# The causal mask as GpSimd selections instead of TensorE products, two score tiles moved forward, and scatters one at a time

## The chip, the cores and the metric

One core of a Trainium2 chip runs the whole kernel in one launch. The metric is the device time of one execution in microseconds; lower is better. The core's engines are named as in the profile: PE (TensorE, matrix products, with PEld for its weight loads), DVE (VectorE), ACT (ScalarE), POOL (GpSimd) and SP, which here issues transfers.

## The reference

It is one layer of attention and one of experts, each behind a layer norm and added to its input, for 8 batches of 1024 tokens of 512 features, in float32.

```python
x = x + attention(layernorm(x))
x = x + experts(layernorm(x))

# attention, 16 heads of 32 features; t is the token's place
theta_q = x_head / (1 + |w_q|) + b_q + t * phi_q      # k alike; v without t
Q = concat(cos theta_q, sin theta_q)                   # K alike; 64 wide
V = cos theta_v + sin theta_v                          # 32 wide
scores = Q K^T / sqrt(64);  scores[key after query] = -inf
out = softmax(scores) V;  result = cos theta_out + sin theta_out

# experts: softmax router over 8, the best 2 of each token, capacity 160 per
# expert and batch (later ones are dropped)
y = relu(rows W1[e] + b1[e]) W2[e] + b2[e]             # 512 -> 2048 -> 512
result[token] = sum over its 2 experts of p * y
```

## The kernel before

**Chunks.** Attention goes through 32 chunks, `n` from 0 to 31. Batch `b` is `n // 4`, head group `c` is `n % 4`; a chunk is four heads of one batch, held as two *pairs* of two heads (the two heads of a pair lie on partitions 0 to 63 and 64 to 127). The features of chunk `n + 1` are computed by DVE and ACT while PE works on chunk `n`.

**Scores.** For a pair, the 1024 queries are cut into two halves `h` of 512. `scores(pair, h, es)` yields one score tile at a time: keys along partitions, queries along the free axis, both heads in one PSUM tile of two banks (`two_banks()`, tiles `ps_s`, of which there are three). Half 0 has three tiles: its first key block with 512 queries; a double tile, in which the key blocks with 384 and with 128 remaining queries share the 512 columns; and one of 256. Half 1 has four full tiles of 512 without a diagonal, and then the same three. Only those last three of each half (`own_keys`) contain a diagonal, and their blocks begin with it. PE makes the scores at L685. The mask is added to them by PE too: at L699 four small bfloat16 products for each such tile add a large negative number where the key lies after the query; the operands `later_b` and `keys_b` are prepared once at the start by GpSimd (L291 to L298). ACT then takes the exponential (L705) and writes the tile `e` to SBUF. The exponentials need no maximum to be subtracted.

**Products.** `attend(n, pr, h, es, halves)` multiplies the tiles `e` of one half by V (L719), tile by tile, into the PSUM tile `av`; V carries a column that gives the sum of the exponentials. After the last tile of a half DVE scales `av` into `av_sb` (L727). `turn(pr, halves, pos)` transposes the two `av_sb` of a pair on PE into a score bank (L215), and DVE divides by the sums (L754, L756) and so fills the chunk's `o_p`.

**The next chunk's features.** `qk_pre` makes the angles of queries and keys (DVE, L526, from a PSUM tile that PE transposed), `angle` wraps them (DVE, L440), ACT squares and takes sines (L444, L447, L586, L595), `times` multiplies them (DVE, L450), and transfers on SP put them into the operand `qk`. The values `v` pass L627, L632, L440 and L450. A chunk's output passes L648, L440, L450 and L659 (its addition to `x_mid`).

**Order.** The program is written in the order in which PE, ACT, DVE and SP are to run it: the helper `some(count, *gens)` takes that many steps from generators of scores (`ahead`) and products (`products`), in their turn. In the middle of a chunk come the last products of pair 0, the router's step, two score tiles of pair 1, and `turn(0, ...)`:

```python
some(NTT, *products)                        # the rest of pair 0
...
route_on(1); route_on(2)                    # the router, in head groups 1 and 2
some(2, *ahead)                             # pair 1: its first two score tiles
turn(0, halves[0], pos_n)
```

GpSimd's instructions are put in order by a scheduler, unless one is pinned with `keep_in_program_order`.

**Router and scatters.** Layer norm and router of batch `b - 1` run in pieces beside batch `b`'s chunks. They end in 16 indirect transfers, which write each token's number to its expert slot in the DRAM table `slot_d` (`scatter`, L770, issued by GpSimd). They are collected in the list `scatters`. For batches 0 to 5 all 16 are issued at one place in head group 3 of the batch that follows, each after the landing of the one before (they write the same table). `fetch_slots` (L1005) reads a finished table back.

**The seam.** After the last chunk come `experts` with the generator `ending()` as an aside: it finishes the last chunk's output, and runs the router of batch 7 while the first experts are computed. The experts' first weights W1 come in quarters; `mix_w1(i, q)` makes four differences of weight blocks (L1173), on GpSimd for the first expert's quarters 0 to 5, then `layer1` uses them in seven products (L1189) per quarter, with DVE combining the results (L1207 to L1222). The scatters of batch 6 (8 + 8) and of batch 7 (16) are issued there, with `together=True`, that is without waiting for one another, each behind the last `mix_w1` written so far.

Of the kernel before, what the change touches and what calls it, by code (L numbers as in the profile page):

```python
# [21 lines left out]
P = 128  # L22
# [43 lines left out]
REACH = [(0, -(-FIRST // CAP)), (FIRST // CAP, B)]  # L66

FAR = 1000.0 * math.sqrt(2 * DH) / (UNIT * UNIT)

# [4 lines left out]
def preln_attn_moe_kernel(  # L74
# [186 lines left out]
    before = own.tile([P, P], F32, name="before")  # L261


    keys_b = own.tile([P, 2, P], BF16, name="keys_b")
    nc.gpsimd.memset(keys_b, 0.0)
    later_b = own.tile([P, 2, P], BF16, name="later_b")
    e_row = own.tile([P, E], F32, name="e_row")
# [16 lines left out]

    later = row2.tile([P, NCH, 2 * P], F32, name="xT", bufs=1)[:, :3, :P]

    def mask():
        for part in range(2):
            for a in range(2):
                r = slice(a * 64, (a + 1) * 64)  # L290
                nc.gpsimd.tensor_copy(later_b[r, part, :], later[r, 1 + part - a, :])  # L291
                nc.gpsimd.tensor_copy(keys_b[r, part, part * 64 : part * 64 + 64], ident[r, r])

    def rest_of_loads():

        nc.gpsimd.memset(later, 0.0)
        for i in range(3):
            nc.gpsimd.affine_select(  # L298
                out=later[:, i, :], in_=later[:, i, :], compare_op=ALU.is_ge, fill=-FAR,
                base=64 * (1 - i), pattern=[[1, P]], channel_multiplier=-1,  # L300
            )
        nc.gpsimd.affine_select(
# [152 lines left out]
    def make_base(c):  # L455
# [4 lines left out]
        )  # L460
        r = room[1]
        if c > 1:
# [47 lines left out]
    def qk_pre(n):  # L510
# [3 lines left out]
        p = qkt.tile([P, 2, S], I32, name="qk_f")  # L514
        r = qkt.tile([P, 2, S], I32, name="qk_r")
        ps = two_banks()
# [159 lines left out]
    def scores(pair, h, es):  # L676

        for parts in tiles_of(h):
            n = sum(w for _, _, w, _ in parts)
            ps = two_banks()  # L680
            own_keys = parts[0][0] >= 4 * h
            for kb, q0, w, at in parts:
                for a in range(2):
                    r = slice(a * 64, (a + 1) * 64)
                    nc.tensor.matmul(  # L685
                        ps[:, a, at : at + w], lhsT=pair[r, 1, kb * P : (kb + 1) * P],
                        rhs=pair[r, 0, q0 : q0 + w], start=at == 0, stop=not own_keys,
                        skip_group_check=True,
                    )
            if own_keys:  # L690

                for part, w in ((0, 64), (1, P)):
                    for a in range(2):
                        r = slice(a * 64, (a + 1) * 64)
                        out_, late = ps[:, a, :w], later_b[r, part, :w]
                        if len(parts) == 2:
                            out_ = ps[:, a, :].rearrange("p (k q) -> p k q", q=P)[:, ::3, :w]
                            late = late.unsqueeze(1).to_broadcast([64, 2, w])
                        nc.tensor.matmul(  # L699
                            out_, lhsT=keys_b[r, part, :], rhs=late,  # L700
                            start=False, stop=part == 1, skip_group_check=True,
                        )

            e = ep.tile([P, 2, n], F32, name=f"e_{n}", bufs=8 if n == 512 else 2)
            nc.scalar.activation(  # L705
                e, ps[:, :, :n], AF.Exp, scale=UNIT * UNIT / math.sqrt(2 * DH)
            )
            es.append(e)
            yield
# [51 lines left out]

    scatters = []
    scattered = {b: [] for b in range(B)}
    mixed = []

    def scatter(count=2 * NTT * TOPK, together=False):

        for _ in range(min(count, len(scatters))):
# [5 lines left out]
            ins = queued.ins  # L774
            if together:
                tc.add_manual_dep(
# [4 lines left out]
                    reason="behind the mixture",  # L781
                )
                for other in scattered[b]:
                    tc.declare_no_dep(ins, other, reason="rows of their own")
            scattered[b].append(ins)

# [567 lines left out]
    rest_of_loads()  # L1354
    mask()
    first_stats(2, NTT)
# [14 lines left out]
    for n in range(NCK):  # L1371
# [220 lines left out]
```

## Time and profile before

| what | value |
|---|---|
| median of 4 runs | 3275.96 us (3274.84 to 3276.7) |
| profiled execution | 3271.5 us |
| its span in the profile | 3269.7 us, granted PE clock 0.997 |
| PE busy | 3190.0 us, 98% |
| DVE busy | 2254.3 us, 69% |
| ACT busy | 1323.1 us, 40% |
| POOL busy | 422.6 us, 13% |
| attention | from 0 to about 1273 us; the experts' first product starts at 1273.24 |
| L685, scores | 3072 products, 601.1 us busy |
| L719, products with V | 3072 products, 524.0 us busy |
| L699, the mask | 1536 products |
| L705, exponentials | 640, 569.6 us busy |
| L770, scatters | 128, mean 1242 ns of one |

Busy time counts overlapping matmuls once. The share of an engine is an average over attention and experts; in attention alone DVE and ACT are busier than in the whole, since the experts leave ACT nearly idle. The four chunks of a batch differ: the head group decides which layer norm and router pieces run beside it.

### The profile page before, as it was taken

How to read it: one execution, taken by the hardware profiler on the slowest of the kernel's cores; microseconds unless marked ns; L12 is line 12 of the kernel's file. 1: busy time of each engine (PE TensorE's matmuls, PEld its weight loads, DVE VectorE, ACT ScalarE, POOL GpSimd, SP SyncE). 2: the span in 40 equal slices, each digit the busy share in tenths (PEclk: the TensorE clock that was granted, in tenths of full speed). 3: DMA queues.
4: the chain of work that ended last, by engine and by line, in shares of the span. 5: the costliest groups of instructions: out<-in, count | busy, mean ns of one | idle time of the engine just before them, and what ended most of it. 6: DMA issues, size and time to landing. Idle time of an engine off the chain costs nothing.

```text
span 3269.7 us, 48752 instructions
## 1 busy us (share of the span) xinstructions
PE 3190.0 (98%) x18942; PEld 2165.8 (66%) x18942; DVE 2254.3 (69%) x4961; ACT 1323.1 (40%) x1617; POOL 422.6 (13%) x387
## 2 busy tenths in 40 slices
PE   5999999999999998999999999999999999999998
PEld 2444444444444444688688688688688688688687
DVE  8887888888788675755755755755755755855854
ACT  7888887888887873211111111211201201201201
POOL 2000202111120212311011011011011011011010
PEclk9999999999999999999999999999999999999999
DMA  5435455453545362323223222322322322322321
GB/s 163 143 98 167 135 146 147 125 156 104 181 123 160 87 175 53 116 55 83 90 50 79 93 52 76 95 52 71 101 49 71 103 47 72 104 47 70 105 42 26
DMA packets 235254, 319.74 MB, mean 98 GB/s; under 512 B 22456, under 2 KB 155280, under 8 KB 222992
## 3 DMA queue, kind: packets, MB, share of 16 engines
q1 hardware_dynamic: 211664, 273.38, 28.5%
q0 software_dynamic: 22912, 43.22, 7.1%
q8 instruction: 150, 2.46, 0.3%
q14 instruction: 80, 0.66, 0.1%
q10 hardware_dynamic: 448, 0.02, 0.0%
HBM read 187.62 MB, written 61.82 MB: 76 GB/s over the span
## 4 chain that ended last, share of the span: by engine, by line
PE 57%; DVE 0%; DMA 0%; issue 0%; POOLq 0%; POOL 0%; DVEq 0%
PE ps_p L1234 29%; PE ps_p L1189 27%; PE ps_t L1135 1%; DMA slots<-slot_d 0%; DMA out_dram<-y,slots 0%; DVE w_t L1068 0%; DVE w L1067 0%; DVE w_t L1066 0%; DVE w_t L1069 0%; POOLq L1588 0%; POOL slot_d L770 0%; POOL slots L1005 0%; DVE y L1250 0%; DVE p L1271 0%; DVE p L1272 0%
## 5 line engine op out<-in xcount | busy, mean ns | idle before, releaser
L705 ACT ACTIVATE e<-ps_s 128x1024 f32<-128x1024 f32 (+1 forms) x640 | 569.6, 938 | 195.3 <-PE ps_s L685 110.8
L685 PE MATMUL ps_s<-qk 64*128 64x512 f32 (+3 forms) x3072 | 601.1, 507 | 37.4 <-DMA qk<-qk_r 12.4
L1234 PE MATMUL ps_p<-w,hid 128*128 128x256 f32 x2560 | 568.7, 380 | 0.0
L1234 PEld LDWEIGHTS ps_p<-w,hid 128*128 128x128 f32 x2560 | 485.2, 191 | 67.0 <-DVE hid L1207 0.5
L719 PE MATMUL av<-e,v 128*64 128x512 f32 (+3 forms) x3072 | 524.0, 490 | 0.0
L1234 PE MATMUL ps_p<-w_t,hid 128*128 128x256 f32 x1920 | 430.3, 379 | 0.9 <-DVE w_t L1068 0.9
L685 PEld LDWEIGHTS ps_s<-qk 64*128 64x128 f32 x3072 | 262.5, 188 | 227.3 <-issue 110.8
L1234 PEld LDWEIGHTS ps_p<-w_t,hid 128*128 128x128 f32 x1920 | 361.3, 190 | 48.5 <-DVE w_t L1068 1.3
L719 PEld LDWEIGHTS av<-e,v 128*64 128x64 f32 x3072 | 200.6, 137 | 284.2 <-issue 268.2
L1189 PE MATMUL ps_p<-xe,w 128*128 128x256 f32 (+1 forms) x1024 | 297.8, 434 | 1.1 <-issue 1.1
L1189 PE MATMUL ps_p<-xe,t 128*128 128x256 f32 (+1 forms) x1024 | 297.1, 433 | 0.9 <-issue 0.9
L1189 PE MATMUL ps_p<-xe_s,t 128*128 128x256 f32 (+1 forms) x1024 | 296.9, 433 | 0.0
L770 POOL DMA_INDIRECT slot_d<-token,slot x128 | 159.0, 1242 | 975.5 <-issue 626.3
L1265 ACT COPY p<-ps_p 128x256 f32<-128x256 f32 x40 | 14.8, 369 | 604.8 <-PE ps_p L1234 604.7
L1189 PEld LDWEIGHTS ps_p<-xe,t 128*128 128x128 f32 x1024 | 194.3, 190 | 82.2 <-issue 1.9
L1189 PEld LDWEIGHTS ps_p<-xe,w 128*128 128x128 f32 x1024 | 193.4, 190 | 82.1 <-DVE hid L1207 3.7
L1189 PEld LDWEIGHTS ps_p<-xe_s,t 128*128 128x128 f32 x1024 | 194.3, 190 | 80.7 <-issue 0.4
L1094 POOL DMA_INDIRECT xg<-xn_d,source x76 | 74.6, 982 | 1074.4 <-PE ps_t L1135 1059.1
L1256 POOL DMA_INDIRECT out_dram<-y,slots x80 | 126.5, 1582 | 624.1 <-DVE y L1251 624.1
L1204 ACT ACTIVATE p<-ps_p,b_t 128x256 f32<-128x256 f32 (+1 forms) x128 | 65.5, 512 | 335.0 <-PE ps_p L1189 180.8
L1221 ACT ACTIVATE hid<-hid,b_more 128x256 f32<-128x256 f32 (+1 forms) x128 | 71.9, 562 | 278.7 <-DVE hid L1220 270.4
L1208 ACT ACTIVATE hid<-hid 128x256 f32<-128x256 f32 (+1 forms) x128 | 60.1, 470 | 299.3 <-DVE hid L1207 291.2
(224 smaller groups left out, 3818.5 us busy)
## 6 DMA issues: line engine op xcount, KB each, us to landing
w<-in_L_ffn_W_dram SPq DMA_DIRECT2D x256, 256.0 KB
w<-in_L_ffn_W_dram SPq DMA_DIRECT2D x64, 512.0 KB
qk<-qk_c SPq DMA_DIRECT2D x124, 256.0 KB
qk<-qk_r SPq DMA_DIRECT2D x124, 256.0 KB
qk_base<-base_d SPq DMA_DIRECT2D x28, 1024.0 KB
xn_d<-xn SPq DMA_DIRECT2D x72, 256.0 KB
x_mid<-in_L_attn_x_dram SPq DMA_DIRECT2D x16, 1024.0 KB
out_dram<-x_mid SPq DMA_DIRECT2D x8, 2048.0 KB
```

Source lines behind the costliest of these rows:

```text
L685: nc.tensor.matmul(ps[:, a, at : at + w], lhsT=pair[r, 1, kb * P : (kb + 1) * P], rhs=pair[r, 0, q0 : q0 + w], start=at == 0, stop=not own ...
L705: nc.scalar.activation(e, ps[:, :, :n], AF.Exp, scale=UNIT * UNIT / math.sqrt(2 * DH))
L719: nc.tensor.matmul(av[a * 64 : (a + 1) * 64, q0 - 512 * h :], lhsT=vt[:, kb, 2 * pr + a, :], rhs=es[i][:, a, at : at + w], start=kb == 0, ...
L770: queued = nc.gpsimd.indirect_dma_start(out=slot_d[b], out_offset=bass.IndirectOffsetOnAxis(ap=idx, axis=0), in_=src, in_offset=None,)
L1094: ins = nc.gpsimd.indirect_dma_start(out=xg, out_offset=None, in_=xn2_d[i % 2], in_offset=bass.IndirectOffsetOnAxis(ap=source[:, e, j0 + j ...
L1135: nc.tensor.transpose(ps[:, c, :], xg[:, c * P : (c + 1) * P], ident)
L1189: nc.tensor.matmul(ps, lhsT=weights[:, k, :], rhs=rows[:, k, :], start=k == 0, stop=k == 1)
L1204: nc.scalar.activation(p1, product(b11, a11), AF.Identity, bias=b1_t[:, e * NHC + q : e * NHC + q + 1])
L1208: nc.scalar.activation(h11, h11, AF.Relu)
L1221: nc.scalar.activation(h12, h12, AF.Relu, bias=more)
L1234: nc.tensor.matmul(ps, lhsT=hs[k][:, part, cols], rhs=ws[k][weight], start=k == 0, stop=k == NHQ - 1,)
L1256: ins = nc.gpsimd.indirect_dma_start(out=out, out_offset=bass.IndirectOffsetOnAxis(ap=meta[:, e, jj[r], 0:1], axis=0), in_=ys[r], in_offse ...
```

## The change

The mask leaves PE. The four products of each own tile go, with their operands and the constants made for them. After the exponential, GpSimd sets e to zero where the key lies after the query, by `affine_select` on the first 128 queries of each block, both heads at once: one selection for a plain tile, two for a double one, 4 per half, 16 per chunk, 512 in all. They are pinned in program order.

The first two score tiles of pair 1 move in front of the last three tiles of products of pair 0: `some(4, *products)`, two tiles of scores, the rest of the products. The router's steps of head groups 1 and 2 now stand directly in front of `turn(0)`.

The scatters of batches 0 to 5 are no longer issued at one place: after the last selection of each half, two of them go (if any are collected), pinned in program order. They are held back during batch 7. In the ending, batch 6's sixteen are issued as 8, 4 and 4, no longer `together`: each waits for the landing of the one before. Batch 7's sixteen stay together. Two tiles of the first chunks' features change their buffers.

```diff
-    keys_b = own.tile([P, 2, P], BF16, name="keys_b")
-    nc.gpsimd.memset(keys_b, 0.0)
-    later_b = own.tile([P, 2, P], BF16, name="later_b")
...
-    def mask():
...
-        nc.gpsimd.memset(later, 0.0)
-        for i in range(3):
-            nc.gpsimd.affine_select(
...
-        r = room[1]
+        r = qkt.tile([P, 2, S], I32, name="qk_r").bitcast(F32) if c == 2 else room[1]
...
-        r = qkt.tile([P, 2, S], I32, name="qk_r")
+        r = room[1].bitcast(I32) if n == 1 else qkt.tile([P, 2, S], I32, name="qk_r")
...
     def scores(pair, h, es):
-        for parts in tiles_of(h):
+        tiles = tiles_of(h)
+        for parts in tiles:
...
-                        rhs=pair[r, 0, q0 : q0 + w], start=at == 0, stop=not own_keys,
+                        rhs=pair[r, 0, q0 : q0 + w], start=at == 0, stop=True,
                         skip_group_check=True,
                     )
-            if own_keys:
-                for part, w in ((0, 64), (1, P)):
-                    for a in range(2):
...
-                        nc.tensor.matmul(
-                            out_, lhsT=keys_b[r, part, :], rhs=late,
-                            start=False, stop=part == 1, skip_group_check=True,
-                        )
             e = ep.tile([P, 2, n], F32, name=f"e_{n}", bufs=8 if n == 512 else 2)
             nc.scalar.activation(
                 e, ps[:, :, :n], AF.Exp, scale=UNIT * UNIT / math.sqrt(2 * DH)
             )
+            if own_keys:
+                for _, _, _, at in parts:
+                    own_ = e[:, :, at : at + P]
+                    tc.keep_in_program_order(
+                        nc.gpsimd.affine_select(
+                            out=own_, in_=own_, compare_op=ALU.is_ge, fill=0.0, base=0,
+                            pattern=[[0, 2], [1, P]], channel_multiplier=-1,
+                        )
+                    )
+            if parts is tiles[-1] and not hold[0]:
+                scatter(2)
             es.append(e)
             yield
...
-    def scatter(count=2 * NTT * TOPK, together=False):
+    def scatter(count=2 * NTT * TOPK, together=False, late=False):
...
-            if together:
+            if together or late:
                 tc.add_manual_dep(ins, mixed[-1].name, ...)
+            if together:
                 for other in scattered[b]:
                     tc.declare_no_dep(ins, other, reason="rows of their own")
+            elif not late:
+                tc.keep_in_program_order(queued)
...
             if b > 1:
                 fetch_slots(b - 2)
-            if b < B - 1:
-                scatter()
+            hold[0] = b == B - 1
...
-        some(NTT, *products)
+        some(4, *products)
         es, halves1 = [[], []], []
         ahead = [scores(pairs[1], h, es[h]) for h in range(2)]
+        some(2, *ahead)
+        some(NTT, *products)
         route_on(1)
         route_on(2)
-        some(2, *ahead)
         turn(0, halves[0], pos_n)
...
     def ending():
         o_st = o_pre(NCK - 1, pos_n)
-        scatter(NTT * TOPK // 2, together=True)
+        scatter(NTT * TOPK // 2, late=True)
...
+        steps = 0
         for name in router(B - 1):
-            if name == "tiles":
-                scatter(together=True)
+            if steps in (0, 3):
+                scatter(NTT * TOPK // 4, late=True)
+            steps += 1
```

More of the change, by code (lines that the diff above doesn't have):

```diff
@@ L66 @@
 REACH = [(0, -(-FIRST // CAP)), (FIRST // CAP, B)]
-FAR = 1000.0 * math.sqrt(2 * DH) / (UNIT * UNIT)
 ROOT_GUESS = float(0x5F3759DF)
@@ L283, in preln_attn_moe_kernel @@
     nc.vector.memset(empty, 0)
-    later = row2.tile([P, NCH, 2 * P], F32, name="xT", bufs=1)[:, :3, :P]
-    def mask():
-        for part in range(2):
-            for a in range(2):
-                r = slice(a * 64, (a + 1) * 64)
-                nc.gpsimd.tensor_copy(later_b[r, part, :], later[r, 1 + part - a, :])
-                nc.gpsimd.tensor_copy(keys_b[r, part, part * 64 : part * 64 + 64], ident[r, r])
-    def rest_of_loads():
-        nc.gpsimd.memset(later, 0.0)
-        for i in range(3):
-            nc.gpsimd.affine_select(
-                out=later[:, i, :], in_=later[:, i, :], compare_op=ALU.is_ge, fill=-FAR,
-                base=64 * (1 - i), pattern=[[1, P]], channel_multiplier=-1,
-            )
+    def rest_of_loads():
         nc.gpsimd.affine_select(
@@ L686, in scores @@
                         ps[:, a, at : at + w], lhsT=pair[r, 1, kb * P : (kb + 1) * P],
-                        rhs=pair[r, 0, q0 : q0 + w], start=at == 0, stop=not own_keys,
+                        rhs=pair[r, 0, q0 : q0 + w], start=at == 0, stop=True,
                         skip_group_check=True,
                     )
-            if own_keys:
-                for part, w in ((0, 64), (1, P)):
[L693 to L699, printed above, removed]
-                            out_, lhsT=keys_b[r, part, :], rhs=late,
-                            start=False, stop=part == 1, skip_group_check=True,
-                        )
             e = ep.tile([P, 2, n], F32, name=f"e_{n}", bufs=8 if n == 512 else 2)
@@ L759, in turn @@
         )
-    scatters = []
+    scatters, hold = [], [False]
     scattered = {b: [] for b in range(B)}
     mixed = []
-    def scatter(count=2 * NTT * TOPK, together=False):
+    def scatter(count=2 * NTT * TOPK, together=False, late=False):
         for _ in range(min(count, len(scatters))):
@@ L1354, in preln_attn_moe_kernel @@
     rest_of_loads()
-    mask()
     first_stats(2, NTT)
```

## The prediction

> **What bounds the kernel now.** I read the busy shares first: PE 3190.0 us of the 3269.7 us span (98%), DVE 69%, ACT 40%, POOL 13%. The change touches attention alone (0 to 1273 us; experts follow) and its seam to the experts, so the shares that count are those of one attention chunk. A table by stage gives four neighbouring chunks (head groups 1, 2, 3, 0); columns: window, then busy us and instructions of PE, PEld, DVE, ACT, POOL, then PE clock, DMA share, GB/s.
>
> ```profile
> 392.30:432.40 40.10, 39.21 (x392) 19.68 (x390) 30.54 (x59) 33.21 (x35) 0.00 (x0) 1.00 0.63 197
> 432.40:468.80 36.40, 36.35 (x312) 17.92 (x308) 31.14 (x69) 32.04 (x33) 0.00 (x0) 1.00 0.51 145
> 468.80:505.50 36.70, 36.09 (x296) 17.64 (x292) 29.85 (x62) 31.76 (x33) 11.30 (x8) 1.00 0.35 87
> 505.50:545.30 39.80, 39.16 (x358) 19.25 (x354) 33.50 (x69) 30.98 (x32) 12.06 (x11) 1.00 0.44 120
> ```
>
> PE is the bound, with no idle time to speak of; but DVE at 31 and ACT at 32 of 36.4 stand close behind it, and GpSimd is nearly empty. So work taken off PE pays only until DVE and ACT stop it.
>
> **Masks off PE.** The answer for the mask line (min/median/max ns of one), and a PE timeline of half a pair's scores (start, duration):
>
> ```profile
> L699 PE MATMUL ps_s<-later_b,keys_b x1536: 189/217/417, 36.4 to 1264.8; 64*128 64x64 bf16 x128, 64*128 64x128 bf16 x64
> ```
> ```profile
> 503.77 0.25 PE L699 MATMUL ps_s<-later_b,keys_b 64*128 64x64 bf16 x4
> 503.85 1.09 PE L685 MATMUL ps_s<-qk 64*128 64x384 f32 x8
> 504.77 0.33 PE L699 MATMUL ps_s<-later_b,keys_b 64*128 64x128 bf16 x4
> 504.94 0.60 PE L685 MATMUL ps_s<-qk 64*128 64x256 f32 x4
> 505.37 0.25 PE L699 MATMUL ps_s<-later_b,keys_b 64*128 64x64 bf16 x4
> 505.46 0.67 PE L215 MATMUL ps_s<-ident,av_sb 64*128 64x64 f32 x16
> ```
>
> Matmuls overlap, so what a mask takes is from its start to the next start: .08 + .17 + .09 = .34 us for each half of a pair. 32 chunks have 128 such halves: **−43.5 us** (1.36 per chunk), all of it on the bound engine.
>
> **The two moved score tiles.** Before, the last products of pair 0 were followed by two score tiles (1.15 + 1.1 us), then by turn(0), which transposes av_sb. These tiles hid L727, which scales the last product into av_sb. After, the tiles stand in front of the last three products, and in 17 of the 31 chunks after the first nothing is left between those and turn(0) (groups 0 and 3, and batch 0). That order, products and then at once turn (there turn(1)), shows at the end of attention:
>
> ```profile
> 1270.72 0.46 PE L215 MATMUL ps_s<-ident,av_sb 64*128 64x64 f32 x8
> 1271.65 0.46 PE L215 MATMUL ps_s<-ident,av_sb 64*128 64x64 f32 x8 [0.46 <-DVE av_sb L727]
> ```
>
> The second eight start .93 after the first and the first issue in .25: .68 us of wait. PE's queue behind it holds the remaining scores, and ACT's exps behind those. 17 × .68 = 11.6. In the other 14 chunks router products (about .85 or .36 us) stand between, but turn(0) then needs a third score bank, free only after the first tile's exp; I take half, .35 × 14 = 4.9. Together **+16.5** (bounds 11.6 and 31 × .68 = 21). Switching between scores and products once more per chunk costs at most .1 us by the spacing of rows like 513.94: **+1** (0 to 3).
>
> **Selections on GpSimd.** 16 per chunk, 256 elements each, between exp and product. No row has one on e; the nearest:
>
> ```profile
> L298 POOL TENSOR_SCALAR_AFFINE_SELECT xT<-xT x3: 284/284/284, 14.1 to 14.6; 128x128 f32<-128x128 f32 x3
> ```
>
> A one-column GpSimd memset takes .09, so .2 for 128 elements more: .48 us each, 7.7 us per chunk on an engine with 24 to 36 free. Products wait for e at least 5 us after its exp, so the selection's length costs nothing; without that cover it would be .48 per masked tile. scatter(2) after a half's last selection blocks GpSimd's queue for two serial scatters (about 5 us); the next selection comes later than that: 0. In batches 0 to 5 scatters already wait for one another in the trace, so spreading them moves nothing else; the gathers and fetches behind them on POOL have tens of us.
>
> What is not free is DVE. DVE's timeline, first beside the GpSimd subtractions L1173 (1307.5 to 1313.7), then without them:
>
> ```profile
> 1312.96 1.11 DVE L1217 SCALAR_TENSOR_TENSOR hid<-u,hid 128x384 f32<-128x384 f32 x1
> ...
> 1326.36 0.56 DVE L1217 SCALAR_TENSOR_TENSOR hid<-u,hid 128x384 f32<-128x384 f32 x1
> ```
>
> It grows from .56 to 1.11 beside a .73-us subtraction; operations that read PSUM keep their .55. POOL pays too: the subtraction of 1281.31 shown further down, issued while DVE's L659 ran (1280.40 to 1281.63), took .90. So I read: whichever runs makes the other wait for its end. DVE work on two SBUF tensors (L450, L627, L632, L648, L659) or a plain scale of one (L440, L414) fills 16.0 of the second window's 36.4 us, 44%, in 13 or so operations. Of 16 selections, 56% start beside none; one of these operations starts within the next .48 in .48 × 13/36.4 = 17% of cases and waits .24 on average: .4 us per chunk. The other 44% wait for DVE and then go first; about half the time the next DVE operation is of the kind and waits .48: 16 × .44 × .5 × .48 = 1.7. So 2.1 us per chunk.
>
> Not all of it is felt. In groups 1 to 3 the loop that matters runs from turn(0) (444.16) over L754, L450, the qk transfers and L440 to ACT's squares, after which the next exps start (458.00): 13.8 of 36.4 us, so .8 lands on it. That loop and ACT's work to the next turn(0), about 21.3 by the rows, make 35.1; PE's new chunk is 36.4 − 1.36 + .5 = 35.5. .8 less .4 of slack: .4 × 23 chunks = 9. In group 0 DVE runs without a gap from 517 to 543 and PE already waits for its L526 there (.56 at 533.62): 2.1 × 26/39.8 = 1.4 is felt whole, and half of the .9 of masks in that stretch, .45, is not gained: 1.85 × 8 = 15. Together **+24**. Bounds: 0 (all meetings in gaps), and DVE paying every .48: 31.1 + 7.7 = 38.8 in groups 2 and 3, 2.4 over before, 41.2 in group 0, 1.4 over, group 1 none: 16 × 2.4 + 8 × 1.4 = 50 over *before*. I stay with the middle, since it counts the operations that the two rows are of.
>
> The Trainium skill, "SBUF — State Buffer", section "Who interferes with whom", lets a DVE operation with two SBUF inputs contend with any GpSimd operation that reads SBUF, which speaks against this change. No row here shows a selection beside such an operation; were selections exempt, the sum would lack the 9 and 11 of the 15.
>
> Attention in sum: −43.5 + 16.5 + 1 + 24 = −2.
>
> **The seam.** GpSimd's order there becomes: last selection, subtractions of W1 quarter 1, twelve scatters of batch 6, each behind the landing of the one before, then the subtractions of quarter 2, then four more scatters. Before, eight scatters ran together at 1242.89, ahead of quarter 2 at 1281.31. POOL's timeline:
>
> ```profile
> 1091.43 1.01 POOL L770 DMA_INDIRECT slot_d<-token,slot  x1 [3.37 <-DMA slot_d<-token,slot]
> ...
> 1242.89 0.99 POOL L770 DMA_INDIRECT slot_d<-token,slot  x1 [14.55 <-DVE token L982]
> 1281.31 0.90 POOL L1173 TENSOR_TENSOR t<-w 128x256 f32<-128x256 f32 x1 [28.55 <-PE ps_p L1189]
> ```
>
> Serial scatters come 2.36 us apart at the least, 4.4 to 5.8 where DMA is over .6 busy, 3.98 on average (1085.06 to 1145.30); together 1.3 (1244.19 follows 1242.89). The last exps end at 1266.14; .48 and four subtractions (2.8) give 1269.4 for the first scatter. Quarter 2's second weight is there at 1269.4 + 12 pitches + 1.4 or so; PE wants it for its product at 1296.53. Pitch 2.37: 1299, a stall of 2.5. Pitch 3.98: 1318.6, a stall of 22. DMA is quiet to 1280 and .49 to 1.02 busy till 1300, so five at 2.4 and seven at 4.4: 1313.6, a stall of 17. PE's own waits of 4.6 us between 1296 and 1307 (for L813, L882, L830) lie inside it and fall away: 12.5. The next four scatters (16 us) end before PE reaches quarter 3.
>
> Waits also cost clock (columns as in the first table):
>
> ```profile
> 64.00:68.00 4.00, 4.00 (x26) 1.77 (x24) 0.34 (x1) 2.09 (x3) 0.00 (x0) 0.55 0.98 238
> 1252.00:1256.00 4.00, 2.50 (x6) 0.95 (x8) 0.95 (x2) 1.96 (x3) 0.76 (x1) 0.51 0.01 1
> ```
>
> After a wait of 3.73 us (58.8 to 62.5) PE got .55 of its clock: 1.8 us lost. After waits of 1.03 and 2.28 it got .51. So **+14** for the seam (bounds 0 and 20).
>
> The page "TensorE: Matmul & The Clock Gate", Part 1, halves the clock after an idle window of about 3.4 us. By it the short stall of 2.5 would cost no clock; by the row of 1252 it can.
>
> **Sum** against the profiled execution of 3271.5 (span 3269.7): −2 + 14 = +12, 3283.5. The median of the runs, 3275.96, lies 4.5 above that execution: **3288**.
>
> **Rivals.** (1) Faster: selections fall on DVE's waits and on operations that read PSUM, and the scatters stay near 2.4: −43.5 + 16.5 + 1 + 2.5 = −23.5, 3252.5. For it: 5 us of DVE idle per chunk and a quiet DMA at 1270. It decides once DVE's loss and the seam together stay below 19.5. (2) DVE becomes the bound: every selection costs it .48; +50 and the seam 14: 3340. It decides once more than some 60% of the selections' time lands on DVE ((35.8 − 31.1)/7.7). Against it: 2.1 of 7.7 by the count above. (3) The same: contention as counted, but the scatters quick: −2 + 2.5, 3276.5.
>
> **Chances.** Forecast .45, (1) .28, (3) .17, (2) .10. A measurement of this kernel tells about 0.2% (6.5 us) from no change. Faster .28, same .17, slower .55. The range reaches down into (1), to 3256, and up past the seam's bound with half of (2)'s surplus, to 3324.
>
> **What would show it.** Right: no L699; L215 of turn(0) waiting .5 to .7 on L727; chunks of groups 2 and 3 at 35.4 to 36.3; L450 above 2.4 on average; the product after 1296 waiting over 8 us on POOL. Wrong: chunks below 35.2 with L450 still 2.28 (then faster); chunks above 37 with DVE over 95% (rival 2); selections far over .5 us; batch 6's first scatter far from 1269.

## The result and the profile after

The changed kernel takes 3276.39 us (median of 40 runs), the kernel before 3273.79 us in runs beside it (60 runs): ratio 1.0008, 95% interval 1.0004 to 1.0012. So +2.6 us, where +12 had been forecast. The profiled execution after took 3277.26 us, its span is 3275.5.

The page shows what the change said. PE's instructions fall from 18942 to 17406 and its busy time from 3190.0 to 3164.1 us; POOL's busy time rises from 422.6 to 726.1. The table by stage, for the same four chunks (columns as before the change: window, then PE, PEld, DVE, ACT, POOL busy, PE clock, DMA share, GB/s):

```profile
390.80:430.40 39.60, 38.38 (x338) 18.66 (x336) 30.66 (x59) 32.80 (x35) 13.93 (x21) 1.00 0.67 203
430.40:466.70 36.30, 35.93 (x260) 16.49 (x258) 30.80 (x67) 31.51 (x33) 11.38 (x17) 1.00 0.50 146
466.70:502.70 36.00, 35.02 (x240) 16.14 (x240) 31.13 (x64) 31.48 (x33) 15.60 (x21) 1.00 0.37 88
502.70:543.90 41.20, 38.59 (x306) 17.88 (x304) 35.87 (x70) 31.00 (x32) 19.75 (x25) 1.00 0.42 114
```

PE has lost 0.4 to 1.1 us of work per chunk. Yet in these four chunks only groups 1 and 3 are shorter, by 0.5 and 0.7 us, and group 0, where DVE now works 35.87 instead of 33.50 us, is 1.4 us longer. Averaged over six batches (the table of the experiments), groups 2 and 3 are as long as before to within 0.1 us, group 1 is 0.3 us shorter, and group 0 is 1.0 us longer.

The wait for L707 (L727 before) at turn(0) in such a chunk is the one that the prediction read from the end of attention (PE's timeline):

```profile
513.51 0.46 PE L213 MATMUL ps_s<-ident,av_sb 64*128 64x64 f32 x8
514.44 0.46 PE L213 MATMUL ps_s<-ident,av_sb 64*128 64x64 f32 x8 [0.46 <-DVE av_sb L707]
```

The line of the selections (min/median/max ns; then who waited):

```profile
L680 POOL TENSOR_SCALAR_AFFINE_SELECT e<-e x512: 398/408/2472, 38.7 to 1258.2; 128x256 f32<-128x256 f32 x171
...
  PEld av L699: 14.1, 43
```

Alone a selection takes .41 us (.48 had been estimated). The longest take about as long as a DVE operation: GpSimd waits for it, and DVE in its turn for GpSimd. DVE's and POOL's timelines in group 0:

```profile
515.84 2.28 DVE L428 SCALAR_TENSOR_TENSOR qk_r<-qk_f,qk_r 128x2048 f32<-128x2048 f32 x1
...
524.74 0.17 DVE L346 TENSOR_TENSOR rstd_t<-rstd_t,rstd_v 128x8 f32<-128x8 f32 x1
...
525.79 0.32 DVE L346 TENSOR_TENSOR rstd_t<-rstd_t,rstd_v 128x8 f32<-128x8 f32 x1
```
```profile
516.16 2.23 POOL L680 TENSOR_SCALAR_AFFINE_SELECT e<-e 128x256 f32<-128x256 f32 x1 [0.87 <-ACT e L672]
...
525.62 1.70 POOL L680 TENSOR_SCALAR_AFFINE_SELECT e<-e 128x256 f32<-128x256 f32 x4
```

The selection at 516.16 ends .27 us after L428 does; the small operation grows from .17 to .32 while four selections run. DVE's longest operations did not grow. The prediction's L450, which is L428 after the change, before and then after (us busy, mean ns of one, from 124 to 1198 us):

```profile
L450 DVE SCALAR_TENSOR_TENSOR qk_r<-qk_f,qk_r 128x2048 f32<-128x2048 f32 x28 | 63.9, 2284 | 0.0
```
```profile
L428 DVE SCALAR_TENSOR_TENSOR qk_r<-qk_f,qk_r 128x2048 f32<-128x2048 f32 x28 | 63.9, 2282 | 0.0
```

And the seam, POOL's timeline and then PE's:

```profile
1261.61 1.01 POOL L750 DMA_INDIRECT slot_d<-token,slot  x1 [0.16 <-issue]
...
1282.84 0.97 POOL L750 DMA_INDIRECT slot_d<-token,slot  x1 [7.21 <-DMA slot_d<-token,slot]
...
1301.07 0.97 POOL L750 DMA_INDIRECT slot_d<-token,slot  x1 [1.41 <-DMA slot_d<-token,slot]
1302.06 0.74 POOL L1156 TENSOR_TENSOR t<-w 128x256 f32<-128x256 f32 x1
```
```profile
1303.65 2.93 PE L1172 MATMUL ps_p<-xe_s,t 128*128 128x384 f32 x4 [13.83 <-POOL t L1156]
```

Twelve scatters take from 1261.61 to 1302, one of them after 7.21 us of waiting, and PE stands 13.83 us for the subtraction behind them. Its granted clock is then .50 from 1303.6 to 1308.0 and .84 in the next 4 us.

### The profile page after: what moved, and what is told of

The parts are those of the page before. It is cut to its first block, busy times and chain, and to the rows that moved or that the text cites. A ratio compares the mean times of both kernels' runs of the same rounds, so it can differ in the third digit from the quotient of the medians.

```text
span 3275.5 us, 46288 instructions
## 1 busy us (share of the span) xinstructions
PE 3164.1 (97%) x17406; PEld 2119.4 (65%) x17406; DVE 2281.1 (70%) x4961; ACT 1309.7 (40%) x1617; POOL 726.1 (22%) x886
## 4 chain that ended last, share of the span: by engine, by line
PE 61%; DVE 2%; DMA 1%; issue 1%; ACT 0%; POOL 0%; SPq 0%; POOLq 0%; DVEq 0%; ACTq 0%
PE ps_p L1217 29%; PE ps_p L1172 29%; PE av L699 1%; PE ps_s L665 1%; PE ps_t L1118 1%; DMA slot_d<-token,slot 1%; DMA qk<-qk_r 0%; ACT e L672 0%; PE ps_s L213 0%; POOL slot_d L750 0%; DMA out_dram<-y,slots 0%; DVE qk_r L428 0%; SPq L589 0%; DVE av_sb L707 0%; DVE qk_r L418 0%
## 5 line engine op out<-in xcount | busy, mean ns | idle before, releaser
L672 ACT ACTIVATE e<-ps_s 128x1024 f32<-128x1024 f32 (+1 forms) x640 | 556.8, 941 | 187.9 <-PE ps_s L665 179.5
L665 PE MATMUL ps_s<-qk 64*128 64x512 f32 (+3 forms) x3072 | 565.7, 501 | 36.8 <-DMA qk<-qk_r 12.4
L699 PE MATMUL av<-e,v 128*64 128x512 f32 (+3 forms) x3072 | 530.6, 491 | 1.8 <-POOL e L680 1.8
L680 POOL TENSOR_SCALAR_AFFINE_SELECT e<-e 128x256 f32<-128x256 f32 x512 | 319.5, 647 | 574.2 <-ACT e L672 573.6
L699 PEld LDWEIGHTS av<-e,v 128*64 128x64 f32 x3072 | 197.6, 137 | 279.8 <-issue 251.9
L1172 PEld LDWEIGHTS ps_p<-xe_s,t 128*128 128x128 f32 x1024 | 195.2, 191 | 95.2 <-POOL t L1156 14.3
L750 POOL DMA_INDIRECT slot_d<-token,slot x128 | 149.2, 1166 | 214.9 <-DMA slot_d<-token,slot 189.8
```

The lines of the kernel that those rows point to most:

```text
L665: nc.tensor.matmul(ps[:, a, at : at + w], lhsT=pair[r, 1, kb * P : (kb + 1) * P], rhs=pair[r, 0, q0 : q0 + w], start=at == 0, stop=True, s ...
L672: nc.scalar.activation(e, ps[:, :, :n], AF.Exp, scale=UNIT * UNIT / math.sqrt(2 * DH))
L680: nc.gpsimd.affine_select(out=own_, in_=own_, compare_op=ALU.is_ge, fill=0.0, base=0, pattern=[[0, 2], [1, P]], channel_multiplier=-1,)
L699: nc.tensor.matmul(av[a * 64 : (a + 1) * 64, q0 - 512 * h :], lhsT=vt[:, kb, 2 * pr + a, :], rhs=es[i][:, a, at : at + w], start=kb == 0, ...
L750: queued = nc.gpsimd.indirect_dma_start(out=slot_d[b], out_offset=bass.IndirectOffsetOnAxis(ap=idx, axis=0), in_=src, in_offset=None,)
L1172: nc.tensor.matmul(ps, lhsT=weights[:, k, :], rhs=rows[:, k, :], start=k == 0, stop=k == 1)
```

## The experiments

The theory at this point was the prediction's own sum: masks off PE −43.5, the moved tiles +17.5, selections +24, the seam +14. The rivals: the gain is not there because DVE and ACT pace the chunks; the moved tiles help rather than cost; the price of a selection is the products' wait for it and not DVE's loss.

One table holds the numbers that the sections below compare. A chunk's length is counted from the first transpose of one turn(1) to that of the next, in the profiled execution of each kernel, and averaged for chunks 4 to 27 (six of each group). "Seam" runs from the last turn(1) to the first product of the second expert layer. "Against before" is the median less that of the kernel before on the same chip, whose number is beside it; in the first two rows it is that of the result, for which no chip is on record.

| kernel | groups 0, 1, 2, 3 | chunk 31 | seam | against before | ratio | chip |
|---|---|---|---|---|---|---|
| before | 40.07, 40.08, 36.39, 36.03 | 33.5 | 94.0 | | | |
| after | 41.07, 39.74, 36.38, 36.12 | 26.3 | 108.4 | +2.6 | 1.0008 | |
| seam_undone | 41.15, 39.77, 36.38, 36.11 | 26.3 | 96.1 | −9.3 | 0.9969 | 0 |
| order_undone | 41.71, 40.45, 36.90, 36.20 | 27.1 | 103.7 | +16.8 | 1.0047 | 0 |
| seam_order_undone | 41.71, 40.49, 36.92, 36.20 | 27.1 | 95.5 | +7.4 | 1.0017 | 0 |
| no_select | 39.70, 39.30, 36.31, 36.21 | 26.3 | 95.2 | −26.9 | 0.9913 | 0 |
| before_no_mask | 39.07, 39.16, 35.55, 34.99 | 31.9 | 94.9 | −34.3 | 0.9893 | 6 |
| before_move | 40.67, 40.37, 37.16, 36.68 | 31.7 | 97.7 | +15.2 | 1.0049 | 6 |
| no_mask_square | 39.08, 40.29, 35.79, 35.07 | 32.8 | 94.8 | −20.2 | 0.9932 | 6 |
| hybrid | 40.53, 39.93, 36.53, 36.28 | 26.3 | 93.8 | −4.7 | 0.9988 | 6 |
| load_early | 40.00, 40.08, 35.62, 35.82 | 25.8 | 91.0 | −15.4 | 0.9953 | 10 |
| select_twice | 45.73, 43.10, 36.89, 36.57 | 26.3 | 89.9 | +62.1 | 1.0188 | 10 |
| select_aside | 40.83, 40.05, 36.51, 36.12 | 26.3 | 90.6 | +1.9 | 1.0005 | 12 |
| after_2 | 41.17, 39.79, 36.38, 36.11 | 26.3 | 102.3 | +13.2 | 1.0039 | 15 |
| no_mask_2 | 38.84, 39.16, 35.55, 35.15 | 27.1 | 92.5 | −28.2 | 0.9910 | 15 |
| no_mask_move | 39.63, 39.30, 36.32, 36.23 | 26.3 | 90.4 | −9.0 | 0.9970 | 15 |
| load_early_2 | 40.26, 39.62, 35.62, 35.80 | 25.8 | 90.2 | −16.0 | 0.9954 | 15 |
| seam_apart | 40.87, 39.34, 36.34, 43.28 | 26.3 | 91.1 | +38.5 | 1.0116 | 10 |
| load_early_apart | 39.87, 39.14, 35.61, 42.59 | 25.8 | 91.2 | +17.9 | 1.0052 | 10 |
| before_later | 39.78, 40.07, 36.38, 36.12 | 27.5 | 97.1 | +3.3 | 1.0007 | 12 |

The median of the kernel before was 3276.01 on chip 0, 3273.18 on 6, 3264.59 on 10, 3260.49 on 12 and 3260.54 on 15. Differences of a few microseconds are therefore taken between kernels of one chip where there are such, and a comparison across chips is called one.

### The seam

seam_undone: the ending as in the kernel before.

```diff
-        scatter(NTT * TOPK // 2, late=True)
+        scatter(NTT * TOPK // 2, together=True)
...
-            if steps in (0, 3):
-                scatter(NTT * TOPK // 4, late=True)
+            if name == "tiles":
+                scatter(together=True)
```

> The changed kernel, but batch 6's sixteen scatters stand as before: 8 + 8, not waiting for one another. If the wait of the third product at 1303.65 (13.83 us on POOL L1156) is the price of the serial scatters and nothing takes its place: 10 to 14 us less than the changed kernel, ratio to before about 0.9965. If PE's old waits in that stretch (4.6 us for L813, L882, L830) and a later one take its place: under 5 us less, ratio about 0.9995 or more.

The ratio falls from 1.0008 to 0.9969 (0.9957 to 0.9981), and the seam from 108.4 to 96.1 us, with the attention part unchanged (it ends at 1262.8 and 1262.2). On one chip, order_undone and seam_order_undone differ by the same edit alone: 9.4 us. The serial scatters cost 9 to 12 us, and nothing took their place.

### The moved tiles

order_undone puts the two tiles behind the last products, seam_order_undone does this in seam_undone:

```diff
-        some(4, *products)
+        some(NTT, *products)
...
-        some(2, *ahead)
-        some(NTT, *products)
         route_on(1)
         route_on(2)
+        some(2, *ahead)
```

> The changed kernel, but the two score tiles of pair 1 behind the last products again, as before. If the move costs what the prediction said (16.5 us, of which PE's waits for L707 at turn(0) show 7.9 and those for ACT 4.3): 8 to 16 us less than the changed kernel, ratio to before 0.996 to 0.998. If DVE and ACT bound the chunks anyway: within 4 us of the changed kernel. If the move gives ACT its scores earlier and so pays: 5 us or more slower, ratio above 1.0023.

> Both undone: only the mask's move to GpSimd and the scatters two at a time are left. If the two parts are independent, it is the sum of the two differences. If masks taken off PE pay in full and selections cost DVE 24 us: about 20 us less than before, ratio 0.994. If DVE's growth (21.6 us by the trace) is felt wholly and PE's 43.5 are only half gained: ratio about 1.000.

Undoing the move makes the kernel slower, by 16.7 us from seam_undone to seam_order_undone. By the prediction it should have given 16.5 back. seam_order_undone, at 1.0017, is also slower than both of its expectations. ACT's timeline of order_undone, in the middle of a chunk, shows why:

```profile
441.03 1.99 ACT L425 ACTIVATE t_r<-t_r 128x1024 f32<-128x1024 int32 x2
445.23 1.28 ACT L672 ACT_TABLE_LOAD   x1 [2.21 <-PE ps_s L665]
446.53 2.48 ACT L672 ACTIVATE e<-ps_s 128x1024 f32<-128x1024 f32 x3
```

The same place before the change:

```profile
438.65 1.99 ACT L447 ACTIVATE t_r<-t_r 128x1024 f32<-128x1024 int32 x2
440.66 1.28 ACT L705 ACT_TABLE_LOAD   x1
442.62 2.75 ACT L705 ACTIVATE e<-ps_s 128x1024 f32<-128x1024 f32 x3 [0.68 <-PE ps_s L699]
```

In these traces ACT loads a table (1.28 us) each time it goes from sines to exponentials. Before, it did so while the scores were still being made, and the exponential waited. With the selections, the buffer of e was last written by GpSimd, so the exponential waits for two engines, and the built program puts one of the two waits on the table load:

```
before:  LoadActFuncSet                  Activation [waits PE]
after:   LoadActFuncSet [waits PE]       Activation [waits Pool]
```

The load then starts only when the first score tile is ready. The traces agree: in order_undone the load stands behind a wait for PE's semaphore and the exponential behind one for GpSimd's; in the kernel before, the load has no wait. Moving that tile forward takes this wait away again. The loads at the exponential's line in a whole trace, with the idle time ahead of them in the last field, before, in order_undone and in the changed kernel:

```profile
L705 ACT ACT_TABLE_LOAD x33 | 42.3, 1283 | 5.4 <-PE ps_s L699 4.9
```
```profile
L672 ACT ACT_TABLE_LOAD x33 | 42.3, 1283 | 57.9 <-PE ps_s L665 57.9
```
```profile
L672 ACT ACT_TABLE_LOAD x33 | 42.3, 1283 | 3.2 <-PE ps_s L665 2.6
```

load_early tests it: seam_order_undone and one exponential of one column, which needs nothing, ahead of the last products.

```diff
+        nc.scalar.activation(warm, ones[:, :1], AF.Exp)
         some(NTT, *products)
```

> seam_order_undone (selections, old order, seam as before) with one more instruction per chunk: an exponential of one column, ahead of pair 0's last products, so that ACT's table load no longer stands behind the wait for the first score tile. If that wait (1.4 to 2.1 us ahead of the load in order_undone, 0.02 in the changed kernel) is what the old order loses with selections: 25 to 40 us less than seam_order_undone, ratio about 0.992 to 0.995, below seam_undone. If the old order loses by something else, the delay of the selections or the products: within 8 us of seam_order_undone, ratio about 1.001.

```profile
430.62 1.99 ACT L426 ACTIVATE t_r<-t_r 128x1024 f32<-128x1024 int32 x2
432.61 1.28 ACT L1468 ACT_TABLE_LOAD   x1
433.90 0.20 ACT L1468 ACTIVATE warm<-ones 128x1 f32<-128x1 f32 x1
434.72 2.48 ACT L673 ACTIVATE e<-ps_s 128x1024 f32<-128x1024 f32 x3 [0.61 <-PE ps_s L666]
```

The load stands where it stood before the change (the 32 loads of L1468 have 0.2 us of idle time ahead of them in all), and group 0 falls from 41.71 to 40.00, group 2 from 36.92 to 35.62. The ratio is 0.9953 (0.9939 to 0.9966) against 1.0017 for the same kernel without that instruction. The two ran on different chips. By these ratios it is some 21 us, less than the expected 25 to 40; in the two traces attention ends 30.4 us earlier (1279.42 and 1249.05). Either way the cause is shown: one column of work, which does nothing else, takes the old order's loss away.

Does the move itself cost what the prediction said? before_move makes the move in the kernel before, masks on PE.

> The kernel before with the two score tiles moved, the mask still on PE, scatters and seam as before. By the prediction: the waits for L727 at turn(0) cost 16.5 us, ratio 1.005. If DVE and ACT pace the chunk and the earlier scores help ACT: at most 3 us either way, ratio 0.999 to 1.001.

It costs 15.2 us, ratio 1.0049 (1.0035 to 1.0063), close to the 16.5 + 1 of the sum. The waits are also those that were counted: in the changed kernel's trace PE waits at turn(0) 17 times for L707 (7.9 us) and 14 times for a score bank behind ACT (4.3 us).

### Masks off PE

before_no_mask leaves L699 out of the kernel before.

> The kernel before without any mask (L699 and its operands are left out), in its own order and with its own scatters. If PE alone bounds the chunks, as the prediction's first term has it: 43.5 us less, ratio 0.9867, groups 2 and 3 at 35.0 and 34.6 us. If a loop over ACT and DVE turns at about 36 us per chunk anyway: groups 2 and 3 stay within 0.3 of 36.4 and 35.9, ratio 0.993 to 0.996.

The ratio is 0.9893 (0.9878 to 0.9908), 34.3 us less. The chunks shrink by 1.00, .92, .84 and 1.04 us, not by 1.36. So PE is the bound for most of the mask's time but not for all of it. PE's waits for ACT's exponentials (us in all, times, longest), in the kernel before and then here:

```profile
PE ps_s L685 <- ACT e L705: 1.6, 2, 1.0
```
```profile
PE ps_s L685 <- ACT e L691: 7.6, 33, 0.6
```

All of PE's listed waits, from about 125 to 1198 us, add up to 23.0 us here and to 15.1 in the kernel before.

no_mask_square also replaces the exponential by a square, so that ACT loads fewer tables:

> As before_no_mask, and the exponential is replaced by a square, which needs no table of its own, so that ACT loses two table loads of 1.28 us per chunk (the output is another; mask and exponential are left out). If ACT's work paces groups 2 and 3: they fall by 1 us or more against before_no_mask, to about 35.0 or below, 25 to 40 us in all. If PE or DVE paces them: the same as before_no_mask within 5 us.

It is slower than before_no_mask, by 14 us on the same chip, where no more than 5 us had been expected. Of 68 table loads 16 are left, and no group is shorter for it (groups 2 and 3 are .24 and .08 longer): table loads that start in time do not pace the chunks. Why group 1 grew by 1.1 us was not followed up.

### The selections

no_select leaves the selections, and with them the mask, out of the changed kernel:

```diff
-            if own_keys:
-                for _, _, _, at in parts:
...
-                        nc.gpsimd.affine_select(
```

> The changed kernel without any selection: the mask is left out, all else stays. If selections hold up DVE as the prediction counts (24 us): ratio to before about 0.9935. If what holds the chunks is the order and the DVE/ACT loop, not the selections: within 5 us of the changed kernel, ratio 0.999 to 1.001.

It runs at 0.9913 (0.9899 to 0.9926). Without selections ahead of them the scatters of batch 6 come earlier, and the seam is 95.2 us; so the fair neighbour is seam_undone, on the same chip, and the selections cost 17.6 us. In the two traces attention ends 13.1 us apart. Groups 2 and 3 pay nothing (.07 and −.1), group 1 .47, group 0 1.45. DVE's busy time per chunk, summed over chunks 4 to 27, is larger with selections by 1.9 us in group 0, but by only .2, .8 and .3 in groups 1, 2 and 3. What grew most in group 0 are short operations of the layer norm, `xn<-xn,mv,rstd` from .58 to .75 us and `rstd<-rstd_t,rstd` from .18 to .30 on average.

select_aside keeps every selection's reading of e, but writes another tile, so that no product waits for it (out=spare in place of out=own_; the mask is left out):

> seam_undone, but each selection reads e and writes a tile that nobody reads: the mask is left out, and products no longer wait for selections; GpSimd's reads and its place beside DVE stay. If what selections cost is DVE's loss (ports): as seam_undone, group 0 at about 41, ratio 0.996 to 0.998. If it is the products' wait for the selections: as without selections, group 0 at 39.7, ratio 0.990 to 0.992.

Group 0 stays at 40.83, where 41.15 with and 39.70 without selections had been measured on another chip. So most of what the selections cost there is DVE's loss, and the products had time to wait. The ratio, 1.0005, lies outside both expectations; the kernel before is 15 us faster on chip 12 than on chip 0, where the others ran; the median, 3262.38, is 13.3 us above no_select and 4.3 below seam_undone, across chips. select_twice makes each selection a second time:

> seam_undone with every selection made twice (the second changes nothing). If a selection's price is what DVE loses to it, in proportion to the number: another 15 to 25 us, ratio about 1.003, most of it in group 0. If the price is the wait that it puts between exponential and product, or the first meeting only: under 6 us, ratio below 0.999.

That is far more than in proportion: 62 us over before, group 0 at 45.73, group 1 at 43.10, and PE now waits 39.5 us for L680 (17 waits, up to 3.7), where the changed kernel has one wait of 1.8. So the cover that made the selection's own length free is used up by twice as many.

hybrid puts the mask back on PE in group 0 alone (`on_pe[0] = c == 0`), with seam_undone's ending:

> The changed kernel with the seam as before, and the mask on PE in head group 0 alone, where DVE has no free time; selections in the other groups. If what the selections cost lies in group 0 (41.15 us there against 39.70 without any): group 0 at about 40.1 and 6 to 10 us less than seam_undone, ratio about 0.9945. If PE's mask costs there what the selection costs: ratio 0.997.

Group 0 becomes shorter by .62, each other group longer by about .15, and the ratio, 0.9988 (0.9978 to 0.9997), is no better than that of seam_undone, which ran on another chip. The 6 to 10 us that were expected did not come.

### The scatters in the chunks

seam_apart takes away the waits among the scatters of batches 0 to 5 by declaring them independent; load_early_apart does it in load_early.

```diff
-            if together:
-                for other in scattered[b]:
-                    tc.declare_no_dep(ins, other, reason="rows of their own")
-            elif not late:
+            for other in scattered[b]:
+                tc.declare_no_dep(ins, other, reason="rows of their own")
+            if not (together or late):
                 tc.keep_in_program_order(queued)
```

> seam_undone, and the pairs of scatters behind each half no longer wait for one another, so that GpSimd is held 2.6 us by a pair and not 5 to 8. If scatters hold up selections in groups 3 and 0 (in group 0 a selection waits until 525.62 for one): groups 0 and 3 shorter by 0.3 or more, 4 to 10 us less, ratio about 0.995. If those selections have time to wait: the same within 3 us, ratio 0.997.

> Both: the old order with an early table load, the seam as before, and scatters that don't wait for one another. If both act and are independent, it is the sum, ratio 0.988 to 0.993, the fastest here; if the load alone acts, as load_early.

Both are slower than the kernel before, 1.0116 (1.0100 to 1.0131) and 1.0052 (1.0039 to 1.0066), and the reason is not one that was expected. Eight scatters now stand in a row ahead of the selections, and the first waits for its token. POOL's timeline in group 3, and PE's:

```profile
479.32 1.06 POOL L750 DMA_INDIRECT slot_d<-token,slot  x1 [4.11 <-DVE token L964]
...
491.33 3.16 POOL L680 TENSOR_SCALAR_AFFINE_SELECT e<-e 128x256 f32<-128x256 f32 x4
```
```profile
492.48 4.53 PE L699 MATMUL av<-e,v 128*64 128x512 f32 x16 [4.98 <-POOL e L680]
```

Group 3 grows from 36.11 to 43.28 us, while groups 0 and 1 are .3 and .4 us shorter than in seam_undone, across chips. So it does not tell what pairs of scatters without waits would cost. But it prices the cover that the prediction named. In the changed kernel selections also stand directly behind two scatters (those of 488.36 start as the scatter of 487.33 ends), against the prediction's "the next selection comes later than that", and group 3 pays nothing for it (36.11, and 36.21 without selections); behind eight, group 3 is 7 us longer per batch.

### The last chunk

Of the 8.5 us by which attention became shorter in the traces (1270.72 to 1262.19), 7.2 lie in chunk 31 (33.5 to 26.3) and 3.6 in chunk 29 (42.9 to 39.3); all other chunks together became 2.3 us longer. No term had these two. In the kernel before, eight scatters are issued during chunk 31, and DVE's L754 starts 5.9 us after the transposes that it needs. before_later takes those eight out of that chunk (one call of `scatter` in `ending` removed, the next one issues all sixteen):

> The kernel before, with the mask on PE and its own order; only batch 6's first eight scatters are taken out of the last attention chunk and go with the other eight behind the subtractions of quarter 2. If those eight held up the last chunk (DVE's L754 starts 5.9 us after its transposes there, PE waits 1.03, 2.28 and .89): chunk 31 falls from 33.5 to about 27, 3 to 7 us less in all if the seam does not take it back. If the last chunk is short in the changed kernel for another reason: chunk 31 stays at 33 and the ratio at 1.000.

Chunk 31 is 27.5 us, but the ratio is 1.0007 (0.9998 to 1.0016). And this was chip 12, where the kernel before takes 3260.49 and its own chunk 31 is not on record; so the run does not tell whether the eight scatters held anything there. no_mask_2 and before_no_mask are the same kernel, with the eight scatters in chunk 31, and chunk 31 takes 27.1 us on chip 15 and 31.9 on chip 6. DVE on chip 6, then on chip 15:

```profile
1220.82 0.26 DVE L740 RECIPROCAL rec<-ps_s 128x16 f32<-128x16 f32 x1 [6.46 <-remote]
```
```profile
1215.63 0.26 DVE L740 RECIPROCAL rec<-ps_s 128x16 f32<-128x16 f32 x1 [1.65 <-PE ps_s L215]
```

So the hold was seen only with the old placing of the scatters, and not on every chip; every kernel with the new ending or the new order of scatters had 25.8 to 27.1 there, on chips 0, 6, 10, 12 and 15. That the scatters cause it is not shown. What holds DVE is not in the trace, and stays open.

### The sum on one chip

> The changed kernel itself, beside the parts of its sum on one chip. Ratio 0.999 to 1.003; its distance to no_mask_move is what selections and serial seam cost together, 25 to 35 us.

> before_no_mask again (mask left out, old order, old scatters), as the first term on the chip of the others. 30 to 36 us less than before, ratio 0.989 to 0.991; the 43.5 of the prediction would be 0.9867.

> no_mask_2 with the two score tiles moved: the move without masks and selections. If turn(0) waits for L727 and a bank as the prediction counts: 16.5 us more than no_mask_2. If PE has slack by then and the move costs less: 0 to 8 us more.

> load_early again beside the changed kernel. If the move in the changed kernel only repairs a table load that stands behind the wait for scores, and a one-column exponential repairs it cheaper: faster than before and than the changed kernel, ratio 0.993 to 0.997, 12 us or more under after_2.

On chip 15: masks off −28.2; the move on top +19.2 (3232.35 to 3251.50); selections and serial seam on top +22.2 (3251.50 to 3273.70); in all +13.2, ratio 1.0039 (1.0025 to 1.0052). The traces part the last of these: the seam 102.3 − 90.4 = 11.9, the rest in attention. The cheaper repair, load_early_2, is at 0.9954 (0.9940 to 0.9968): 16 us faster than before and 29 faster than the changed kernel. It is the fastest kernel here that keeps the mask. Its order is the old one and after_2 has the moved tiles; in the two traces attention ends 16.8 us apart (1245.96 and 1262.75). So the move does cost what the prediction had for it, once the table load no longer needs it.

## Why the prediction was wrong

The forecast of +12 came out as +2.6 beside the kernel before, and as +13.2 on chip 15. Two things failed in the sum. Its first term, −43.5, "all of it on the bound engine", was too large, since only 28 to 34 us were gained; and so were the +24 of the selections, which cost 10 to 18. These two errors nearly cancel, so that the sum fits on chip 15 is luck: there the masks gave 15 us less than forecast, and selections and seam together cost 16 us less (22.2 for 24 + 14). What brought +12 down to +2.6 beside the kernel before is a loss at the end of attention, which the prediction put at nothing: 10.8 us in chunks 29 and 31 of the traces. Step by step:

- **Masks off PE, −43.5.** Measured −34.3 and −28.2. "All of it on the bound engine" failed. The rows gave 1.36 us per chunk rightly, but the chunks gave back only .84 to 1.04, as PE came to wait more for ACT and DVE (23.0 us for 15.1). The prediction had the limit in hand (DVE and ACT close behind PE), and booked it under the selections instead.
- **The moved tiles, +16.5 and +1.** Measured +15.2 with masks on PE, +19.2 without masks: right in size, and by the waits that were named. What the prediction did not see is what the move is worth: with selections in the old order the table load has to wait, 57.9 us in all, and with that wait the move saves 16.7. Since the forecast is of a kernel in which the tiles are moved, its number did not suffer; but the order of ACT's waits was not looked at, only what PE waits for.
- **Selections, +24.** Measured 17.6 on chip 0, and about 10 on chip 15 (22.2 less a seam of 11.9). DVE's loss of 2.1 us in every chunk came in group 0 alone (1.9); there 1.4 was to be felt, and 1.45 to 1.54 was. In groups 2 and 3 DVE lost .8 and .3, and the chunks nothing, so of the 9 us put in groups 1 to 3 only group 1's came (.47 a chunk for .4). The operations were not the ones counted, either: the 2.28 us of L450, which was to come out above 2.4, did not change; operations of up to 1.2 us grew, and the long ones made the selections wait. Each engine making the other wait was read rightly, and so was the products' time to wait (select_aside).
- **The seam, +14.** By the traces +14.4 (94.0 to 108.4), by kernels 9 to 12. The wait of 13.83 on GpSimd's subtractions stands where it was put. The first scatter came at 1261.61 and not at 1269.4, since attention ended 8.5 us earlier; seen from the last turn(1) it is .6 ahead, where 1.3 had been put. A small slip: the pitch of the serial scatters from 1085.06 to 1145.30 is 4.02 on average, not 3.98, and one of 4.64 (1108.04 to 1112.68) stands where DMA is .02 busy, so a busy DMA is not all that stretches them.
- **What had no term.** Chunks 29 and 31, 3.6 and 7.2 us, in which the kernel before loses time in its trace and the changed kernel does not; without them the profiled pair would lie 16.6 us apart and not 5.8. As far as the traces tell, that makes the difference between +12 and +2.6; why the kernel before loses that time stays open. On chip 15 its median is 3260.54 against 3273.79, and its twin without a mask has no hold in chunk 31 there, but its own trace on that chip is not on record. The range was set around one profiled execution's end of attention, taken as a fixed piece.

Of the rivals, DVE as the bound did not come: its price of 50 would need each selection paid whole, and 10 to 18 were paid. The rival of quick scatters named 3276.5, and 3276.39 was measured, but not by its cause: the scatters were not quick, and PE stood 13.83 us for them.

On the Trainium skill: "SBUF — State Buffer", "Who interferes with whom", has a DVE operation with two SBUF inputs contend with a GpSimd operation that reads SBUF. The runs agree for selections: the L680 of 516.16 took 2.23 us beside L428, and group 0 stays at 40.83 us when the products no longer wait and only the reading beside DVE is left.

## What to carry to other kernels

When a new engine writes into a shared buffer, the next writer of that buffer has one more engine to wait for, and here that second wait put an older one on something that used to run early, a table load. Look at the waits of each engine after the change, not only at the work that moved. Here the bound engine stood at 98% with two others at 85 to 88% of a chunk, and work taken off it gave 65 to 79% of its price; so try such work alone first, by leaving it out. A cheap instruction that pulled the table load forward was worth more here than the reordering that covered it, by 16.8 us.

## What the runs showed that was not expected

The kernel before takes 3260.5 us on some chips and 3276.0 on others. Without its mask it differs by some 5 us in its last chunk alone between chips 6 and 15, where DVE starts late on one and the trace names no engine for it; the rest of the 15 us is not found. The changed kernel's two medians lie 3 us apart (3273.7 and 3276.4). A comparison of 0.1% between two kernels can so depend on the chips that it is made on: 1.0008 over all, 1.0039 on one.
